# An attention and FFN kernel: every second step's probabilities through DRAM, inputs prepared in the FFN's time, first sums on GpSimd

## The chip, the core and the metric

The kernel runs on one core of a Trainium2 chip. The core has five instruction streams that matter here: TensorE (PE, matmuls), VectorE (DVE), ScalarE (ACT), GpSimd (POOL) and SyncE (SP). SP computes nothing in this kernel; its queue issues nearly all the DMA transfers, in order. Each engine runs its own instructions in order and waits on semaphores for the others. The metric is the device time of one execution, in microseconds. The median of three runs of the kernel before is 805.54 us (805.47 to 806.14).

## What is computed

The inputs are x of shape (16, 128, 1024), a context of the same shape, the weights and biases of an attention layer with 32 query heads and 8 key and value heads of 32 elements each, and a 0/1 matrix of 1024 x 1024 with one scale for the FFN. Everything is float32. Cut to what matters:

```python
def xattn(q_in, ctx):                      # q_in = layernorm(x)
    Q = q_in @ Wq + bq                     # 32 heads of 32
    K = ctx @ Wk + bk                      # 8 heads of 32
    V = ctx @ Wv + bv
    scores = einsum("bhgqd,bhkd->bhgqk", Q, K) / sqrt(32)
    w = softmax(scores, axis=-1)           # 128 x 128 for each batch and query head
    y = einsum("bhgqk,bhkd->bhgqd", w, V)
    return y.reshape(B, S, 1024) @ Wo + bo

x = x + xattn(layernorm(x), ctx)
h = layernorm(x); h[..., 819:] *= -4.0     # an inhibitory part, -0.8 / 0.2
x = x + scale * (h @ kernel)
```

## The kernel before

The 16 batches are taken in eight groups of two (`GB = 2`), numbered 0 to 7. For a group the kernel needs: the context turned so that its features lie on the partitions (`cT`), K and V from it, the normalized x turned in the same way (`xT`), Q from it, attention for two batches, the output projection, the norm, and the FFN.

**Attention steps.** A group has four attention steps, 0 to 3: batch of the pair is step mod 2, and `a` (which half of the K and V heads) is step div 2. `attend` writes one step. `scores` puts 16 small matmuls on PE, into four PSUM tiles of 128 queries x 4 heads x 128 keys. For each tile, `exponentials` takes the negated maximum on DVE (L571) and four exponentials with their sums on ACT (L575); `divide` multiplies by the reciprocal of the sums on DVE (L587), giving p. The product with V needs the keys on the partitions, so `turn` transposes p on PE, four matmuls against the identity (L592), and ACT copies the result from PSUM to SBUF (L594). When all four tiles are turned, `weighted` does four matmuls with V (L602), and ACT copies the result to `yT` (L610).

**What fills PE between.** While DVE and ACT work on the softmax of a step, PE works on other matmuls: the output projection of the group before (`out_proj`, tiles o_u, o_v, o_c), `prep_k` and `prep_v` of the next group, `prep_q` of the next group (tiles q_u, q_v, q_c), and `ffn` of the group before (tiles f, two batches). The Q product and the output projection are done with seven half-size products instead of eight (`seven`), from sums of blocks. The sums of weight blocks (`combine`, L781) are formed once, on DVE in group 0, stored to DRAM (L784) and loaded again in each group as pieces. The sums of activation blocks (L635 for the output projection) are formed in each group.

**Weight pieces.** The blocks of Wq and Wo and their sums come as pieces of 512 KB through a ring of eight buffers (`fetch`, L219). The load of a new piece is issued on SP just behind the matmul that has read the piece eight places before.

**Turning x and the context.** A context batch is loaded with its rows already spread over four partition quadrants (L157, four DMAs), and DVE then turns blocks of 32 x 32 (L343). x of groups 2 and up is normalized on DVE (L286, with the power on POOL, L285), stored to DRAM (`through_dram`, L308), loaded back by quadrants (L305) and turned on DVE (L361). The FFN's input goes the same way (`dram_f`, `turn_f`, L719).

**What sets the order.** The order is written out by hand in one Python object, `Stream`. It holds a queue of generators (pieces of dense PE work, each of which yields its nominal microseconds) and a list of events with nominal due times (`later`). `run` takes pieces from the queue until a nominal time and fires events that have come due; what is fired emits its instructions at that place in every engine's order. Nothing is reordered afterwards, so the nominal times decide who stands behind whom on each queue, SP's included. The loop at L891 adds the dense work of each group to the queue and then runs the four steps. In the steady groups (1 to 5): output projection, loads of the context two groups on, K, load of the first residual x, V, Q, FFN of the first batch of the group before, load of the second residual x, FFN of the other batch. The x of the next group is loaded and prepared from the start of the group (`get_x`), its context is turned in the first 18 nominal microseconds (`prep_ctx`). At the end of `ffn` SP stores the batch (L744); the buffer of that x is then reused for a residual load (L173), which therefore waits for the store to land.

## Time and profile before

The profiled execution took 805.76 us; its span, from first to last instruction, is 804.0 us.

| | |
|---|---|
| median of the runs | 805.54 us |
| profiled execution, and its span | 805.76 us, 804.0 us |
| TensorE clock granted | 0.996 |
| PE busy | 773.9 us (96%) |
| DVE busy | 489.1 us (61%) |
| ACT busy | 321.4 us (40%) |
| POOL busy | 71.0 us (9%) |
| one steady group (318.79 to 414.56 us) | 95.77 us, PE busy 94.52 |
| DMA moved | 190.31 MB, mean 237 GB/s |
| SP's queue, busy share of the 16 DMA engines | 72.4% |

In the profile's lines, `out<-in` names the tile written and the tiles read, `x128` is a count of instructions, then come the busy time in microseconds, the mean of one instruction in nanoseconds, and the idle time of the engine just before these instructions, with what ended it. A row of 40 digits shows the span in slices of 20 us, in tenths. In a table of stretches each row is a stretch of time, its length, the busy time and count of each engine, the granted clock, the share of the 16 DMA engines and the rate in GB/s. Timeline lines give the start, the duration, engine, line and operation. PE's instructions overlap each other, so the distance of two starts tells the cost of one better than its duration. One float32 matmul of the program appears as two instructions on PE.

### The profile page before, as it was taken

Reading aid. Unit: us, or ns where it says so; the run is one execution under the profiler, and the core shown is the slowest. Engines: PE = TensorE matmul, PEld = TensorE weight load, DVE = VectorE, ACT = ScalarE, POOL = GpSimd, SP = SyncE. Lnnn points to the kernel's source line nnn. Section 1 sums busy time; section 2 is a strip of 40 time slices with the busy share of each in tenths; the row PEclk is TensorE's granted clock in tenths of the full one; section 3 lists DMA queues with packets and bytes.
Section 4 is the critical chain, followed back from the end, with each engine's and each line's share of the span. In section 5 each row is a group of like instructions: output and inputs, shape, how many; then the busy total and the mean of one; then the engine's idle time right before and its main releaser. Section 6 shows DMA issues by size and latency. Waiting matters only on the chain.

```text
span 804.0 us, 13722 instructions
## 1 busy us (share of the span) xinstructions
PE 773.9 (96%) x5024; PEld 574.4 (71%) x5024; DVE 489.1 (61%) x910; ACT 321.4 (40%) x1257; POOL 71.0 (9%) x109
## 2 busy tenths in 40 slices
PE   3998999999999999999999999999999999999998
PEld 3886795589846897479864798548984689646556
DVE  1369756756487564866647575675647856567442
ACT  0143674344334352344433444334434445466100
POOL 1000003010010201001010100102001010100300
PEclk9999899999999999999999999999999999999999
DMA  9999499888488983889659984689847867562511
GB/s 204 360 312 319 155 372 393 265 252 270 143 283 271 249 263 140 305 252 283 208 188 293 271 264 156 244 263 261 263 158 270 293 198 260 181 214 74 197 45 79
DMA packets 98355, 190.31 MB, mean 237 GB/s; under 512 B 7888, under 2 KB 57040, under 8 KB 98288
## 3 DMA queue, kind: packets, MB, share of 16 engines
q1 hardware_dynamic: 96480, 187.73, 72.4%
q10 hardware_dynamic: 1664, 1.57, 1.1%
q8 instruction: 40, 0.66, 0.3%
q0 software_dynamic: 144, 0.14, 0.1%
q14 instruction: 27, 0.22, 0.1%
HBM read 160.04 MB, written 29.36 MB: 236 GB/s over the span
## 4 chain that ended last, share of the span: by engine, by line
PE 76%; DVE 12%; DMA 6%; issue 3%; SPq 1%; POOL 1%; ACT 0%; ACTq 0%; POOLq 0%; DVEq 0%
PE f L317 15%; PE q_u L442 13%; PE o_u L653 9%; PE q_v L442 6%; PE v L317 6%; PE tpp L592 6%; PE k L317 5%; PE o_v L653 5%; PE sc L559 4%; PE av L602 4%; PE q_c L442 3%; DVE p L587 2%; DVE st_a L277 2%; DVE x L667 2%; DVE cT L343 2%
## 5 line engine op out<-in xcount | busy, mean ns | idle before, releaser
L575 ACT ACTIVATE p<-sc,negm 128x128 f32<-128x128 f32 x512 | 181.0, 368 | 152.8 <-DVE negm L571 91.6
L594 ACT COPY pt<-tpp 128x512 f32<-128x512 f32 x128 | 74.6, 589 | 139.7 <-PE tpp L592 139.2
L571 DVE TENSOR_REDUCE negm<-sc 128x4 f32<-128x512 f32 x128 | 86.9, 681 | 38.2 <-PE sc L559 37.5
L317 PE MATMUL f<-wf_sb,x2l 128*128 128x512 f32 x256 | 105.4, 412 | 0.0
L575 ACT ACTIVATION_READ_ACCUMULATOR p<-sc,negm 128x1 f32 x512 | 105.2, 205 | 0.0
L317 PE MATMUL f<-wf_sb,x2h 128*128 128x512 f32 x256 | 101.1, 395 | 0.0
L587 DVE TENSOR_TENSOR p<-p,inv 128x512 f32<-128x512 f32 x128 | 89.8, 701 | 4.4
L179 POOL TENSOR_TENSOR x<-x,bo_b 128x256 f32<-128x256 f32 x64 | 50.2, 815 | 376.4 <-DMA x<-in_x_dram 318.5
L592 PE MATMUL tpp<-ident,p 128*128 128x128 f32 x512 | 76.8, 275 | 6.1 <-DVE p L587 4.0
L592 PEld LDWEIGHTS tpp<-ident,p 128*128 128x128 f32 x512 | 62.6, 142 | 27.6 <-issue 18.1
L442 PE MATMUL q_u<-t,piece 128*128 128x128 f32 x672 | 80.9, 275 | 0.0
L442 PEld LDWEIGHTS q_u<-t,piece 128*128 128x128 f32 x672 | 77.9, 192 | 0.0
L317 PE MATMUL v<-wv_sb,cT 128*128 128x256 f32 x256 | 63.0, 397 | 12.1 <-DMA wv_sb<-in_L_xattn_Wv_dram 12.1
L737 DVE SCALAR_TENSOR_TENSOR x<-f,fscale,x 128x512 f32<-128x512 f32 x32 | 24.0, 750 | 75.0 <-PE f L317 74.9
L653 PE MATMUL o_v<-piece,s 128*128 128x512 f32 x128 | 60.8, 601 | 2.9 <-DVE x L667 2.9
L653 PE MATMUL o_u<-piece,s 128*128 128x512 f32 x128 | 59.6, 598 | 3.4 <-DVE x L667 3.4
L317 PEld LDWEIGHTS v<-wv_sb,cT 128*128 128x128 f32 x256 | 49.6, 201 | 18.6 <-issue 12.1
L653 PE MATMUL o_u<-piece,yT 128*128 128x512 f32 x128 | 58.5, 599 | 0.0
L317 PE MATMUL k<-cT,wk_sb 128*128 128x256 f32 x256 | 57.8, 379 | 0.0
L317 PEld LDWEIGHTS f<-wf_sb,x2l 128*128 128x128 f32 x256 | 48.2, 188 | 10.9 <-issue 1.1
L317 PEld LDWEIGHTS f<-wf_sb,x2h 128*128 128x128 f32 x256 | 48.2, 188 | 10.3 <-issue 0.5
L317 PEld LDWEIGHTS k<-cT,wk_sb 128*128 128x128 f32 x256 | 48.0, 190 | 8.9 <-issue 2.6
(82 smaller groups left out, 911.9 us busy)
## 6 DMA issues: line engine op xcount, KB each, us to landing
piece<-o SPq DMA_DIRECT2D x64, 512.0 KB, 4.4
piece<-q SPq DMA_DIRECT2D x56, 512.0 KB, 5.9
piece<-in_L_xattn_Wq_dram SPq DMA_DIRECT2D x50, 512.0 KB, 5.8
piece<-in_L_xattn_Wo_dram SPq DMA_DIRECT2D x48, 512.0 KB, 4.5
xn<-in_x_dram SPq DMA_DIRECT2D x16, 512.0 KB, 5.4
x<-in_x_dram SPq DMA_DIRECT2D x16, 512.0 KB, 4.9
ctx<-in_ctx_dram SPq DMA_DIRECT2D x60, 128.0 KB, 7.3
out_dram<-x SPq DMA_DIRECT2D x15, 512.0 KB, 3.0
```

The lines of the kernel that those rows point to most:

```text
L179: lambda cut=cut: nc.gpsimd.tensor_add(x_t[:, cut], x_t[:, cut], bo_b[:, cut]) and None,
L317: nc.tensor.matmul(mm, lhsT=lhsT, rhs=rhs, start=k == 0, stop=k == n - 1)
L442: nc.tensor.matmul(mm if part is None else mm[:, part], lhsT=lhsT, rhs=rhs, start=start and n == k == 0, stop=k == len(some) - 1, skip_gro ...
L559: nc.tensor.matmul(tiles[i][:, g], lhsT=qT[rows, g], rhs=kT[rows, a, cols], start=True, stop=True,)
L571: nc.vector.tensor_reduce(negm, tile_, AX.X, ALU.max, negate=True)
L575: nc.scalar.activation(p[:, g], tile_[:, g], AF.Exp, bias=negm[:, g : g + 1], accum_out=total[:, g : g + 1],)
L587: nc.vector.tensor_mul(p, p, inv.unsqueeze(2).to_broadcast([P, NG, S]))
L592: nc.tensor.transpose(tp[:, g], p[:, g], ident)
L594: nc.scalar.copy(pt, tp)
L602: nc.tensor.matmul(mm[i * HD : (i + 1) * HD], lhsT=vs[b][:, h * HD : (h + 1) * HD], rhs=pts[i], start=True, stop=True,)
L653: nc.tensor.matmul(mm, lhsT=lhsT[:, 2 * k + c], rhs=w[:, c], start=start and k == c == 0, stop=k == c == 1, skip_group_check=True,)
L737: nc.vector.scalar_tensor_tensor(x_t[:, cut], mm, fscale, x_t[:, cut], ALU.mult, ALU.add)
```

## The change

It has three parts and the retiming that goes with them.

1. In groups 1 to 6, steps 1 and 3 don't turn p on PE. The exponentials are written so that two tiles lie interleaved in blocks of 32 keys; DVE divides and then turns 32 x 32 blocks in place; the two tiles of a pair are stored to DRAM in one DMA (`store_blocks`) and loaded back into `pT_all` with four (`fetch_blocks`), all on SP. The weighted sum of such a step is emitted 4 nominal us into the next step. A step of this kind runs for its nominal length less 1.9 us, the others for their length less 2.0. p and its transpose lie in one buffer each (`p_all`, `pT_all`) in all steps. The output projection's sums are formed in another order, s3 first, since y of step 3 now comes late.
2. The x of the group after the next is loaded, normalized and sent through DRAM in the FFN's time, step 3 (`get_x`, `rows_x`), and its context is turned there; only the last turn of x (`turn_rows`) is left for the next group. Due times of the FFN's input (`FBACK`, `late`) are moved.
3. Of the four rounds of first sums, three are formed on POOL, one stays on DVE. In group 0, Wv and Wk are loaded in two halves, the norms of x are placed among the Q product's pieces, and half of the DVE copies of the first Q are moved to ACT.

The core of the diff:

```diff
     def load_by_quadrants(dst, w, queues):
...
-        for k in range(NB):
-            queues[k % len(queues)].dma_start(out=dst[k * 32 : (k + 1) * 32], in_=src[k])
+        for h in range(2):
+            cut = slice(h * NC // 2, (h + 1) * NC // 2)
+            for k in range(NB):
+                queues[k % len(queues)].dma_start(
+                    out=dst[k * 32 : (k + 1) * 32, cut], in_=src[k][:, cut]
+                )
...
+    def rows_x(b):
...
+        normalize(by_quadrant(row), by_chunk(src), stats, f"a{b}")
+        through_dram(row, f"x{b}", 2.5, 7.0, 7.0, lambda c_t: rows.update({b: c_t}))
...
+    p_all = const.tile([P, NI, NG * S], FP, name="p_all")
+    pT_all = const.tile([P, NP, NK, 2, NG * HD], FP, name="pT_all")
+    p_dram = dram.tile([NP, NK, P, 2 * NG * HD], FP, name="p_dram")
...
+    def turn_blocks(i):
+        p = probabilities(i, True).rearrange("p g t k -> p t g k")
+        nc.vector.transpose(p, p)
+
+    def store_blocks(pair):
+        p = p_all[:, 2 * pair : 2 * pair + 2].rearrange("p i n -> p (i n)")
+        nc.sync.dma_start(
+            out=p_dram[pair].rearrange("t p n -> p t n"),
+            in_=p.rearrange("p (t n) -> p t n", t=NK),
+        )
+        stream.later(4.0, lambda: fetch_blocks(pair))
+
+    def fetch_blocks(pair):
+        for t in range(NK):
+            nc.sync.dma_start(
+                out=pT_all[t * HD : (t + 1) * HD, pair].rearrange("r k i n -> r k (i n)"),
+                in_=p_dram[pair, t].rearrange("(k r) n -> r k n", r=HD),
+            )
...
-                (1.0, 1, "a22", "a21", ADD),
-                (2.5, 2, 1, "a11", SUB),
-                (7.0, 3, "a11", "a21", SUB),
-                (9.5, 4, "a12", 2, SUB),
+                (2.0, 3, "a11", "a21", SUB),
+                (5.6, 1, "a22", "a21", ADD),
+                (6.0, 2, 1, "a11", SUB),
+                (10.0, 4, "a12", 2, SUB),
...
+                def by_vector():
+                    divide(b, a, i, total, True)
+                    turn_blocks(i)
+                    if i % 2 == 1:
+                        stream.later(2.5, lambda: store_blocks(i // 2))
...
-    def combine(w, k, part):
+    def combine(w, k, part, engine=nc.gpsimd):
...
-                nc.vector.tensor_tensor(dst[:, cols], left[:, cols], right[:, cols], op)
+                engine.tensor_tensor(dst[:, cols], left[:, cols], right[:, cols], op)
...
+        def turn_rows(grp):
+            for n, at in enumerate((30.0, 32.0, 34.0, 36.0)):
+                stream.later(at, lambda n=n: turn_x(grp * GB + n // 2, n % 2))
...
                 stream.add(
-                    once(get_x, nxt),
-                    once(prep_ctx, nxt, 3.7, 8.0, 13.0, 18.0),
+                    once(turn_rows, nxt),
                     os[grp - 1],
                     once(get_ctx, nxt + 1),
                     prep_k(nxt),
                     once(load_residual, b0, 4.0),
                     prep_v(nxt),
                     qs[nxt],
+                    once(get_x, nxt + 1),
+                    once(prep_ctx, nxt + 1, 2.5, 7.0, 11.0, 16.0),
                     ffn(p0),
                     once(load_residual, b1, 2.0),
                 )
...
-                pts = attend(b, a, length)
+                via_dram = not first and q % 2 == 1
+                us = length - 1.9 if via_dram else length
+                pending = attend(b, a, us, via_dram)
+                us -= 0.0 if via_dram else 2.0
...
+                if via_dram:
+
+                    stream.later(4.0, lambda b=b, a=a: weighted(b, a) or 1.2)
+                else:
+                    weighted(b, a)
+                    stream.now += 1.0
```

## The prediction

> **What bounds the kernel now.** I read the page first: the busy line, then the slices, then the groups that the diff touches.

> ```profile
> span 804.0 us, 13722 instructions
> PE 773.9 (96%) x5024; PEld 574.4 (71%) x5024; DVE 489.1 (61%) x910; ACT 321.4 (40%) x1257; POOL 71.0 (9%) x109
> ...
> PE   3998999999999999999999999999999999999998
> ...
> DMA  9999499888488983889659984689847867562511
> ...
> L587 DVE TENSOR_TENSOR p<-p,inv 128x512 f32<-128x512 f32 x128 | 89.8, 701 | 4.4
> ...
> L592 PE MATMUL tpp<-ident,p 128*128 128x128 f32 x512 | 76.8, 275 | 6.1 <-DVE p L587 4.0
> ```

> PE is busy 96% of the span, in every slice but the first, so PE's instruction stream is the time: a matmul taken away counts in full as long as nothing that PE needs comes late. The transposes of p (L592) are such matmuls. VectorE has room; the DMA row is near 9 in many slices and is what to distrust. I therefore cut one steady group into its four steps, from score matmuls to score matmuls:

> ```profile
> core 0: us, PE busy (x) PEld busy (x) DVE busy (x) ACT busy (x) POOL busy (x), PEclk, DMA share, GB/s
> 318.79:342.34 23.55, 22.30 (x70) 9.92 (x69) 20.01 (x37) 8.31 (x36) 2.29 (x4) 1.00 0.90 306
> 342.34:365.35 23.01, 23.01 (x136) 17.05 (x132) 13.67 (x28) 9.85 (x39) 1.09 (x2) 1.00 0.89 250
> 365.35:388.60 23.25, 23.25 (x232) 22.17 (x228) 16.55 (x28) 10.77 (x41) 4.01 (x4) 1.00 0.91 286
> 388.60:413.38 24.78, 24.78 (x176) 20.46 (x172) 10.77 (x19) 9.09 (x38) 0.98 (x2) 1.00 0.41 138
> ```

> PE has no gap in steps 1 to 3. The DMA engines are about full in steps 0 to 2 and only 0.41 busy in step 3, the FFN's time. The price of a transpose is read from PE's timeline in step 1:

> ```profile
> 354.74 0.60 PE L592 MATMUL tpp<-ident,p 128*128 128x128 f32 x4
> 355.18 1.03 PE L317 MATMUL k<-cT,wk_sb 128*128 128x256 f32 x4
> ```

> Four transposes hold PE 0.44 us, start to next start (the durations overlap, so their sum misleads).

> **The change, part by part.** The sum starts from the profiled execution's 805.8 us: 804.0 of span and 1.8 around it. The median of the runs shown, 805.5, is 0.3 below, less than matters here. A difference under 0.2% (1.6 us) can't be told from none.

> *Transposes removed.* By the order of the changed program, steps 1 and 3 of groups 1 to 6 lose their L592 rows (512 become 320): 12 steps x 4 tiles x 0.44 = **-21.1**. That certainty is why "the change does nothing" is no rival. ScalarE loses 48 copies of 0.59 us, worth nothing (40% busy, PE never waited long for it).

> *Added on VectorE.* 48 block transposes; the nearest row, turn_f L719, took 0.70 for the same shape, so 2.8 us a step, in steps with 23.0 - 13.7 = 9 and 14 us free: nothing by itself. The new access patterns (exponentials written in runs of 32, a product over 4x128, the copies of pT and yT) have no row; x2h L720, just as broken up, took 0.63 against 0.59 for the plain copy, so I take 0, with at most 0.1 us for each of 16 exponentials, 1.6 us a step, on an engine with half its time free.

> *The first group.* VectorE forms all first sums now, and PE waits for it there:

> ```profile
> PE tpp L592 <- DVE p L587: 4.0, 2, 3.4
> ```

> With 24 of 32 adds on GpSimd these 4.0 us go. GpSimd needs about 1.5 us for 512 elements (L179: 5.72 us for 7 of 256), so the three rounds take 36 us; their stores must be back before the q and o products read them, near 92 us and later, and they are begun around 44. GpSimd's power for the layer norm now queues behind up to two adds, 3 us, and VectorE behind that; VectorE has that slack once its own adds are gone. The other price shows in the timelines at 128 us, VectorE first, then GpSimd:

> ```profile
> 128.02 1.13 DVE L635 TENSOR_TENSOR s<-yT,yT 128x512 f32<-128x512 f32 x1
> ```
> ```profile
> 125.83 5.72 POOL L179 TENSOR_TENSOR x<-x,bo_b 128x256 f32<-128x256 f32 x7 [0.63 <-DMA x<-in_x_dram]
> ```

> A two-input VectorE instruction beside GpSimd took 1.13, where its like takes 0.69. [...] I take the row: VectorE saves 24 x 0.65 = 16 us in that group. Splitting Wv's load in halves lets v begin on the first half (it waited until 12.1 for all of it, and k then until 19.3 for Wk); v's end, and with it the norm of x, comes some 1.3 us sooner; the bounds are 0 and 3. Together **-5.3**.

> *What the removed matmuls covered: the handover.* Each pair of tiles now goes VectorE, store on SP's queue, landing, four fetches, landing, and only then may the weighted sum run. It stands a little into the next step, and everything on PE is queued behind it. Two rates: 512 KB lands alone in 3.0 us (out_dram, median), behind other transfers in 5.4 (dram_f) and four fetches of 128 KB in 4.8 (turn_f). [...] The queues are loaded, so I take the rows, and full engines at 306/0.90 = 340 GB/s.

> Step 1 (t from its scores): PE has scores 1.1, 8 o matmuls 6.9, k and v 13.8, scores 1.1, 14 q matmuls 3.1, so it wants pair 0 at 26.0 and pair 1 at 26.5. VectorE turns tiles 1 and 3 by about 9.4 and 15.6 (0.69 and 0.70 for each product and transpose, the o reads and the xT transposes between). On SP, four weight pieces (released at 2.8 to 8.0) and eight ctx loads stand ahead, each waiting for a lane that an earlier transfer holds; before, the ctx loads held SP 9.05 us; with dram_x and turn_x gone from this step, they end near 12. Store 0 at 12.2 lands 15.8; fetches to 17.6; store 1 at 17.7 lands 21.5; fetches 21.5 to 22.8, behind x and dram_f, land at 26.4 to 27.5. Late by 0 to 1: 0.5, six times, **+3.0**.

> Step 3, groups 2 to 5: scores, 32 q matmuls, 64 f matmuls at 0.233, scores, 4 o matmuls: pair 0 wanted at 27.7, pair 1 at 28.2. Here the diff also puts two x loads, two stores and eight fetches of x. Bytes: 138 GB/s x 24.8 us = 3.4 MB, +3.1 of x, +2.1 of p = 8.6 MB, which full engines move in 25 us. The empty step becomes full. Tiles 1 and 3 are turned by 8.2 and 14.2. Store 0 (9.5, behind two pieces and two x loads) lands 16.4; fetches; store 1 at 18.1 lands 21.8. Then SP stands at out_dram, which waits for VectorE's FFN read at about 18, now behind the x norm; the residual load behind it waits until out_dram has landed (23.3: before it was issued 3.7 us after it); then dram_x; then the fetches, 24.2 to 25.8, landed at 30. Late by **1.8**, four times: **+7.2**. In group 1 out_dram stands ahead of the fetches of pair 0 too, and there are 8 q matmuls fewer: wanted 26.5, landed 31.5: **+5.0**. Group 6 has one FFN batch, no ctx loads and no x loads: 0.

> What is late next: while PE stands, ScalarE holds yT's copy ahead of the next exponentials and VectorE the first o sum; by their rows the sums are still done 2 us before PE wants them. The weight pieces go out up to 6 us late behind turn_x; the ring of 8 pieces at 1.72 us gives 13.8, less 5 for landing. ctx and x of the next group are ready earlier than before; they were never waited for.

> Sum: 805.8 - 21.1 - 5.3 + 3.0 + 7.2 + 5.0 = **795**.

> **Rivals.** (a) *All handovers fit.* For it: step 3's share is only 0.41 now, stores alone land in 3.0, and 1.8 us is within the error of such a walk. Against: the byte count of step 3. Time: 805.8 - 26.4 = 779.
> (b) *Handovers clearly late, slower.* One mechanism: the SP queue serves in order, and the second fetch waits for out_dram's landing (step 3) or the ctx lanes (step 1). Each microsecond of mean lateness costs 12; from 26.4/12 = 2.2 us on, the change loses. At 3.2 us it is 818, at 4 it is 827. For it: shares of 0.9 in the neighbouring steps; against: PE's standing lets the transfers catch up, so lateness doesn't pile up.
> (c) *The weights starve.* If the 6 us delay and full engines use up the ring's margin, PE also waits at o pieces in step 0, some 2 us in each of five groups: 805, no change. Against it: 4 us of margin left by the above.

> **How the numbers follow.** Chances: the forecast (787 to 803) 0.40; (a) 0.22; (b) 0.29; (c) 0.09. Faster: 0.40 + 0.22 + a little of (c) = 0.63; within 0.2%: 0.04, mostly (c); slower: 0.33. The range reaches from 776, (a) with 3 us more from the start, to 818 in (b).

> **What would show it.** L592's successor at 320 transposes; PE's gap before av in steps 1 and 3 released by the pT_all DMA, under 1 us in step 1, about 2 in step 3 and 5 in group 1; a steady group of about 94.5 us instead of 95.8; DMA share about 0.9 in step 3; no wait for VectorE's p in the first 130 us. The forecast is wrong if those gaps are absent (779) or above 2.2 us in the mean, if PE waits for pieces, or if PE waits for VectorE beside GpSimd's adds in the first group.

## The result, and the profile after

The changed kernel takes 874.98 us (median of 4 runs, 869.47 to 881.08) where the kernel before takes 805.84: a ratio of 1.086, 95% interval 1.079 to 1.093. The prediction said 795 and a range to 818. The profiled execution took 881.1 us, its span is 879.3 us, 75.3 more than before.

From the page of the changed kernel: busy times, the slices of PE, of its granted clock and of DMA, and the groups that answer to those shown of before.

```profile
span 879.3 us, 13494 instructions
...
PE 795.8 (90%) x4832; PEld 573.4 (65%) x4832; DVE 517.3 (59%) x930; ACT 293.2 (33%) x1213; POOL 105.8 (12%) x133
...
PE   5988778998979899898998989899897999999998
...
PEclk9997979999989999898999989989998999999999
DMA  9988679779587897988879797797977977873321
...
L618 DVE TENSOR_TENSOR p_all<-p_all,inv 128x512 f32<-128x512 f32 x128 | 91.0, 711 | 4.4
...
L654 PE MATMUL av<-pT_all,v 128*32 128x512 f32 x256 | 53.4, 653 | 43.4 <-DMA pT_all<-p_dram 41.8
...
L624 PE MATMUL tpp<-ident,p_all 128*128 128x128 f32 x320 | 48.4, 276 | 10.3 <-DVE p_all L618 10.3
```

Two rows of the kernel before, for comparison:

```profile
PEclk9999899999999999999999999999999999999999
...
L602 PE MATMUL av<-pt,v 128*32 128x512 f32 x256 | 36.6, 605 | 0.0
```

The transposes did go from 512 to 320, and the division in its new access pattern cost nothing (711 ns, 701 before). But PE now stands (is idle, waiting) 43.4 us ahead of av, where it did not wait at all before: 3.6 us in the mean at the 12 handovers. And PE's busy time *rose*, from 773.9 to 795.8, although it has 21 us less to do by the prediction's price. The clock row says why: it has 8s and 7s where it had one 8 before (0.953 granted over the span, 0.996 before).

One steady group cut into its four steps, with the columns of the prediction's table:

```profile
351.28:381.02 29.74, 26.28 (x105) 11.29 (x104) 14.39 (x26) 8.73 (x37) 2.76 (x4) 0.89 0.94 288
381.02:403.03 22.01, 22.01 (x120) 16.13 (x116) 15.46 (x31) 7.33 (x35) 0.55 (x1) 1.00 0.76 220
403.03:433.26 30.23, 26.74 (x225) 22.97 (x224) 16.00 (x28) 9.98 (x39) 3.73 (x5) 0.89 0.90 270
433.26:457.90 24.64, 23.68 (x168) 20.02 (x164) 19.67 (x37) 7.53 (x35) 1.09 (x2) 1.00 0.73 236
```

Steps 1 and 3 are shorter or as long as before (23.0 and 24.8); what is lost stands in the steps behind them, 0 and 2, where the handover is waited for: 30 us instead of 24.7 (of which the table of before leaves out the first 1.2) and 23.3. In each of the two, 3.5 us is standing, and the clock is 0.89. PE's timeline at one of them shows both:

```profile
404.11 3.39 PE L450 MATMUL q_u<-xT,piece 128*128 128x128 f32 x28
407.43 1.05 PE L654 MATMUL av<-pT_all,v 128*32 128x512 f32 x4
411.97 1.92 PE L654 MATMUL av<-pT_all,v 128*32 128x512 f32 x4 [3.49 <-DMA pT_all<-p_dram]
413.82 1.22 PE L450 MATMUL q_u<-xT,piece 128*128 128x128 f32 x4
...
428.16 0.61 PE L450 MATMUL q_u<-t,piece 128*128 128x128 f32 x4
```

The same four matmuls with V take 1.05 us for pair 0 and 1.92 for pair 1, after 3.49 us of standing; four q matmuls take 1.22 behind it and 0.61 later. SP's queue in the same step 1 (start, time on the queue, DMA), whose scores began at 381.02:

```profile
394.46 0.31 SPq L157 DMA_DIRECT2D ctx<-in_ctx_dram  x1
395.08 0.39 SPq L636 DMA_DIRECT2D p_dram<-p_all  x1
399.76 1.73 SPq L644 DMA_DIRECT2D pT_all<-p_dram  x4
401.61 0.38 SPq L636 DMA_DIRECT2D p_dram<-p_all  x1
402.03 0.50 SPq L178 DMA_DIRECT2D x<-in_x_dram  x1
402.63 0.97 SPq L313 DMA_DIRECT2D dram_f<-x2n  x1
405.46 2.01 SPq L644 DMA_DIRECT2D pT_all<-p_dram  x4
```

By t from the scores, with the prediction's walk in brackets: last ctx load 13.4 (12), store 0 14.1 (12.2), second fetch 24.4 (21.5), landed 30.9 (26.4 to 27.5). Each link is a little later than in the walk, and it adds up to 3.4 to 4.5 us. Step 3, from 433.26:

```profile
442.22 2.13 SPq L173 DMA_DIRECT2D xn<-in_x_dram  x2
444.45 0.38 SPq L636 DMA_DIRECT2D p_dram<-p_all  x1
452.60 1.75 SPq L644 DMA_DIRECT2D pT_all<-p_dram  x4
454.46 0.38 SPq L636 DMA_DIRECT2D p_dram<-p_all  x1
454.95 0.44 SPq L805 DMA_DIRECT2D out_dram<-x  x1
459.38 0.34 SPq L178 DMA_DIRECT2D x<-in_x_dram  x1
459.77 0.43 SPq L313 DMA_DIRECT2D dram_x<-xq  x1
460.29 2.70 SPq L644 DMA_DIRECT2D pT_all<-p_dram  x4
```

Store 0 left at 11.2 (9.5) and took 8.1 us to land beside the two x loads; the second fetch, behind out_dram and the residual load that waits for it, left at 27.0 (24.2) and landed at 34.0 (30). Last, what PE waits for by releaser, where the last three rows, nearly all of them in the first 155 us, are waits that the prediction had excluded or not seen:

```profile
PE av L654 <- DMA pT_all<-p_dram: 41.8, 11, 5.4
PE tpp L624 <- DVE p_all L618: 10.3, 3, 9.7
...
PE k L322 <- DVE cT L348: 7.1, 2, 4.4
PE o_u L714 <- DVE s L696: 3.6, 1, 3.6
```

### The profile page after: what moved, and what is told of

It is laid out like the page before. It is cut to its first block, busy times and chain, and to the rows that moved or that the text cites. A ratio compares the mean times of both kernels' runs of the same rounds, so it can differ in the third digit from the quotient of the medians.

```text
span 879.3 us, 13494 instructions
## 1 busy us (share of the span) xinstructions
PE 795.8 (90%) x4832; PEld 573.4 (65%) x4832; DVE 517.3 (59%) x930; ACT 293.2 (33%) x1213; POOL 105.8 (12%) x133
## 4 chain that ended last, share of the span: by engine, by line
PE 48%; DMA 26%; DVE 8%; issue 7%; SPq 7%; POOL 3%; ACT 1%; ACTq 0%; POOLq 0%; DVEq 0%
DMA p_dram<-p_all 11%; PE o_u L714 9%; PE q_u L450 7%; PE o_v L714 6%; DMA pT_all<-p_dram 5%; PE f L322 5%; PE q_v L450 4%; PE av L654 4%; SPq L644 4%; PE o_c L714 4%; PE tpp L624 3%; PE q_c L450 3%; DMA out_dram<-x 2%; PE sc L567 2%; DMA ctx<-in_ctx_dram 2%
## 5 line engine op out<-in xcount | busy, mean ns | idle before, releaser
L600 ACT ACTIVATE p_all<-sc,negm 128x128 f32<-128x128 f32 x512 | 180.9, 371 | 279.9 <-DVE negm L597 212.4
L597 DVE TENSOR_REDUCE negm<-sc 128x4 f32<-128x512 f32 x128 | 86.5, 677 | 41.8 <-PE sc L567 41.8
L600 ACT ACTIVATION_READ_ACCUMULATOR p_all<-sc,negm 128x1 f32 x512 | 107.3, 210 | 0.0
L618 DVE TENSOR_TENSOR p_all<-p_all,inv 128x512 f32<-128x512 f32 x128 | 91.0, 711 | 4.4
L654 PE MATMUL av<-pT_all,v 128*32 128x512 f32 x256 | 53.4, 653 | 43.4 <-DMA pT_all<-p_dram 41.8
L625 ACT COPY pT_all<-tpp 128x512 f32<-128x512 f32 x80 | 46.7, 590 | 108.0 <-PE tpp L624 105.9
L322 PE MATMUL v<-wv_sb,cT 128*128 128x256 f32 x256 | 61.0, 396 | 9.4 <-DMA wv_sb<-in_L_xattn_Wv_dram 9.4
L322 PE MATMUL k<-cT,wk_sb 128*128 128x256 f32 x256 | 61.4, 401 | 7.1 <-DVE cT L348 7.1
L322 PEld LDWEIGHTS k<-cT,wk_sb 128*128 128x128 f32 x256 | 51.5, 202 | 18.3 <-DVE cT L348 8.1
L624 PE MATMUL tpp<-ident,p_all 128*128 128x128 f32 x320 | 48.4, 276 | 10.3 <-DVE p_all L618 10.3
L624 PEld LDWEIGHTS tpp<-ident,p_all 128*128 128x128 f32 x320 | 38.9, 143 | 27.8 <-issue 25.4
L322 PEld LDWEIGHTS f<-wf_sb,x2h 128*128 128x128 f32 x256 | 48.7, 190 | 10.8 <-issue 0.2
```

The costliest lines, as they stand in the source:

```text
L322: nc.tensor.matmul(mm, lhsT=lhsT, rhs=rhs, start=k == 0, stop=k == n - 1)
L597: nc.vector.tensor_reduce(negm, tile_, AX.X, ALU.max, negate=True)
L600: nc.scalar.activation(p[:, g], tile_[:, g].rearrange("p (t k) -> p t k", t=NK), AF.Exp, bias=negm[:, g : g + 1], accum_out=total[:, g : g ...
L618: nc.vector.tensor_mul(p, p, factor)
L624: nc.tensor.transpose(tp[:, g], p_all[:, i, g * S : (g + 1) * S], ident)
L625: nc.scalar.copy(pT_all[:, i // 2, :, i % 2].rearrange("p k (g q) -> p g k q", g=NG), tp.rearrange("p g (k q) -> p g k q", k=NK),)
```

## The experiments

Theory H: the loss is part 1's, at each handover a stand and the slow clock after it. Rivals: the moved x preparation, or GpSimd's sums, carry it (X); the DMA engines are simply full (B); the order on SP's queue decides (Q). All times are medians; "before" beside them was between 804.4 and 805.4 us in every comparison.

**Which part loses.** Handovers off:

```diff
-                via_dram = not first and q % 2 == 1
+                via_dram = False
```

> Theory H (handover): the loss of 69 us is part 1 alone, because at each of the 12 handovers PE stands about 3.6 us for the pT_all transfer (the groups row of the changed kernel puts 43.4 us ahead of av) and then runs its next matmuls at about half speed, 2 to 2.6 us more. With every step's probabilities turned by PE again and the other two parts kept, the time is what the prediction's sum gives without part 1: about 800 us (796 to 806), and PEclk is 1.0 throughout. Rival X (x preparation moved into step 3, or GpSimd's sums, carry the loss): the time stays above 830 us, with PE waits that no pT_all transfer ends.

823.16 us (1.023 of before, 1.021 to 1.025). So the handovers, with what they do to the rest, cost 51.8 of the 69 us, but neither theory was right: without them the kernel is still 18 us slower than before, where the sum had a gain of 5. PE has no gap over 0.8 us in the steady groups; the loss is in the first group. There VectorE's timeline, and then PE's:

```profile
99.19 0.69 DVE L618 TENSOR_TENSOR p_all<-p_all,inv 128x512 f32<-128x512 f32 x1
107.87 1.29 DVE L282 BATCH_NORM_STATS2 st_a<-xn 128x6 f32<-128x512 f32 x2 [8.00 <-DMA xn<-in_x_dram]
```
```profile
65.48 1.99 PE L322 MATMUL k<-cT,wk_sb 128*128 128x256 f32 x8 [2.77 <-DVE cT L348]
73.38 2.93 PE L322 MATMUL k<-cT,wk_sb 128*128 128x256 f32 x6 [5.91 <-DVE cT L348]
```

VectorE stood 8.00 us at the statistics of the next group's x, whose load took 7.4 us to land, and the softmax of step 3 stood behind it: PE waited 9.4 us for p. Before that, PE waited 8.7 us in all for the turned context, which VectorE turned late, behind sums that were slow beside GpSimd's.

**The two in the first group, one at a time.** The norm of x begun 16 instead of 5 nominal us after its load there, on the kernel without handovers:

```diff
-                    once(get_x, nxt + 1),
+                    once(get_x, nxt + 1, 16.0),
```

> The kernel without handovers (all probabilities turned by PE), with the norm of the next group's x begun 11 us later in the first group alone. Theory V: there VectorE stood 8.00 us at the x statistics for their load, the softmax of step 3 behind it, and PE 9.4 us for p: without that wait the time falls from 823 by 9 to 11 us, to 813. Rival: the wait for x's residual at the start of group 1 grows by as much, and the time stays at 820 or more.

811.89 us: 11.3 less, about as expected. Then the sums on VectorE too. Theory P: beside GpSimd's sums VectorE's are slow (1.6 to 1.7 us instead of 0.64, a norm of x 1.74 instead of 0.81), and this, by holding back cT, is what part 3 loses in the first group:

```diff
-    def combine(w, k, part, engine=nc.gpsimd):
+    def combine(w, k, part, engine=nc.vector):
```

> The same with the first sums on VectorE as well (parts 1 and 3 undone, part 2 kept with its first norm later). Theory P: 4 to 8 us less than with GpSimd's sums, 805 to 809 us, level with the kernel before. Rival (the sums on GpSimd relieve VectorE): 5 us more, 818 us.

805.21 us (1.000 of before, 0.998 to 1.001): 6.7 us less, and level with before. The same edit on the whole changed kernel:

> The changed kernel with the first sums back on VectorE (part 3 undone, parts 1 and 2 kept). [...] Rival, the prediction's own term (GpSimd's sums relieve VectorE): 5 us slower than the changed kernel, about 880 us.

867.14 us, 7.8 less than the changed kernel, against the rival's 880 and as theory P has it, though the runs of both kernels spread over 7 to 12 us; the 6.7 us above is the firmer figure. VectorE's piece sums in the changed kernel, with GpSimd idle and then beside GpSimd's, and GpSimd's own:

```profile
59.09 1.28 DVE L852 TENSOR_TENSOR piece<-piece,piece 128x512 f32<-128x512 f32 x2
...
65.56 3.42 DVE L852 TENSOR_TENSOR piece<-piece,piece 128x512 f32<-128x512 f32 x2
```
```profile
62.60 12.06 POOL L852 TENSOR_TENSOR piece<-piece,piece 128x512 f32<-128x512 f32 x8
```

VectorE formed eight of these sums: the four beside GpSimd's took 6.6 us, the other four 2.6. The slow ones stood ahead of cT; with all sums on VectorE, PE's wait for cT fell from 7.1 to 3.1 us in the changed kernel. So in the first group part 3 loses about 7 us and part 2 (which moves the norm) 11. With these two taken away, what is left of parts 2 and 3, with the retimed sums of the output projection, is level with the kernel before; that this level is a gain and a loss of the same size shows further down.

**One handover at a time.** The condition `q % 2 == 1` becomes `q == 1`, then `q == 3`.

> Probabilities through DRAM in step 1 alone (6 handovers), step 3 turned by PE. Theory H with each handover late by itself: 6 x (3.5 stand + 2.4 slow clock - 1.8 transposes) = +25 us over the kernel without handovers: about 825 us. Rival Q (the lateness is carried from one handover to the next by a queue that never catches up): a handover with a quiet step before it is in time, PE's stand ahead of av is under 1 us, and the time is about 790 us.

> Probabilities through DRAM in step 3 alone (6 handovers, of which the last group's has fewer loads beside it). Theory H: 6 x (3.6 + 2.4 - 1.8) = +25 us over the kernel without handovers, about 825 us, and the two halves add up to the loss of the whole change. Rival Q: under 795 us. If step 3 is worse than step 1 by more than 10 us, the x preparation that now shares its DMA counts.

822.06 and 844.87 us, that is -1.1 and +21.7 against the kernel without handovers. Step 1 alone does no harm (stands of 1.8 us at most, no slow matmul behind them), though it doesn't gain what its transposes were priced at either. That 822 meets the 825 of theory H is chance: 825 was 25 more than an expected 800, and 800 had been 823. Step 3 alone costs nearly what theory H says (+25), and together they cost 31 us more than the two apart. By PE's timeline, step 1 begins with 6 matmuls of the output projection when it is alone and with 8 in the whole change: a late av takes PE's planned time in step 0, and two matmuls slip into step 1 (read from the order; this shift was not tried by itself). With them a fourth weight piece stands on SP's queue ahead of the ctx loads (three before), so that store 0 leaves at 14.1 instead of 12.5, and the second fetch lands at 30.9 instead of 27.6. That is 3 us, but it costs more than that: stands of 1.2 to 1.8 us had no slow clock behind them, and five of the six in the changed kernel (2.1 to 4.1 us) had (where the clock fell is told in the last section).

**The slow clock by itself.** 32 useless transposes on PE ahead of every late weighted sum, into the tile that it writes afterwards (`warm` is 32 behind a handover and 0 elsewhere):

```diff
+        for n in range(warm):
+            at = mm[:, n % NK].rearrange("p g q -> p (g q)")
+            nc.tensor.transpose(at, ident, ident)
```

> The changed kernel with 32 useless transposes of the identity on PE ahead of each late weighted sum (12 places, about 3.5 us each, written where av is written afterwards): PE works where it stood. Theory C (the slow matmuls after a stand are the clock gate's answer to idling): the stands shrink to under 1 us, the matmuls after them take their usual time, and the kernel becomes faster although it does 42 us more work: about 875 - 12 x 2.3 = 847 us. Rival (the slow clock has another cause, transfers or power): the matmuls stay slow, and the time is 875 us or more.

864.55 us: faster than the changed kernel by 10 us with 42 us more work on PE (12 x 3.5, an estimate). Theory C holds in kind: the granted clock is back at 0.990, at half only in the first group, and the matmuls behind the handover take their usual time (eight with V 1.06 us, four q 0.61). The size missed (847 expected): the useless work and the 10.8 us that PE still stood are together 11 us more than the 41.8 us of stands that they replace. That an unslowed PE asks for the next handover sooner would explain it, but wasn't tested.

**SP's order or full engines.** Stores and fetches from ScalarE's queue (the store due 3.5 nominal us after its turn instead of 2.5, the fetch 5 after the store instead of 4):

```diff
-        nc.sync.dma_start(
+        nc.scalar.dma_start(
...
-            nc.sync.dma_start(
+            nc.scalar.dma_start(
```

> The changed kernel with the stores and fetches of the probabilities issued from ScalarE's queue instead of SP's. Theory Q (SP's queue serves in order: store 0 stands behind weight pieces and ctx loads, the second fetch behind out_dram, the residual load and dram_f): store 0 leaves within 1 us of its turn, PE's stand ahead of av falls under 1 us in step 1 and under 2 us in step 3, the matmuls after it keep their pace, and the time is about 825 us. Rival B (the DMA engines are full and the transfers themselves are slow): issue is earlier but landing is not, and the time stays above 860 us. ScalarE waits for landings instead, which may hold back exponentials by 1 to 2 us a step.

836.76 us: 38 less, most of the 50 that theory Q expected; the stands ahead of av that a landing ended fell from 41.8 to 17.4 us. (The due times moved too, by 1 us each, and later; that alone would not make a handover earlier.) ScalarE paid with 64.0 us of waiting for landings. Then single moves on SP's queue in the changed kernel. The residual load ahead of k, so that it isn't between store 1 and its fetches; and, in another kernel, 4 us more slack for the weighted sum of step 1:

```diff
+                    once(load_residual, b0, 4.0),
                     prep_k(nxt),
-                    once(load_residual, b0, 4.0),
```
```diff
-                    stream.later(4.0, lambda b=b, a=a: weighted(b, a) or 1.2)
+                    stream.later(8.0 if q == 1 else 4.0, lambda b=b, a=a: weighted(b, a) or 1.2)
```

> The changed kernel with one transfer moved: the residual load of step 1, which stood on SP's queue between store 1 and its fetches, is put ahead of k, so that it leaves before store 0. It asks why step 1's handovers stand 2.8 to 4.1 us here and at most 1.8 us when step 3 has none. Theory Q2 (order on SP's queue; the second fetch landed in 4.9 us behind the x load and in 3.1 without): PE's stands in step 1 fall by about 2 us, most of them under the length from which the slow clock follows, 5 x (2 + 2.4) = 22 us less: about 853 us. GpSimd's residual add also comes earlier, so rs_f and VectorE's x2n wait less. Rival (the DMA engines are too full after step 3's handover whatever the order): 868 us or more.

> The changed kernel with one number changed: the weighted sum of step 1's probabilities is put 8 instead of 4 us into step 2. Its pair 1 lands 30.9 us after the step's scores and is wanted at 26 to 27.4; with 4 us more it is in time. Theory H (a handover costs its stand and the slow clock after it, nothing else): 5 or 6 x (3.4 + 2.4) = 29 to 35 us less, about 842 us, and no slow matmuls in step 2. Rival B (full DMA engines: PE, no longer standing, asks for its weights and for step 3's handover sooner and stands there): 860 us or more.

876.84 and 868.9 us: both missed. In the first, the x load now leaves just ahead of store 0, which takes 5.8 us to land instead of 4.7, and the second fetch lands at 30.3: the contention moved. In the second, PE no longer stands at av but, for as long, at q_c; VectorE and GpSimd at that place:

```profile
504.41 1.20 DVE L291 TENSOR_SCALAR x2n<-x,mv_f,rs_f 128x1024 f32<-128x1024 f32 x1 [11.06 <-POOL rs_f L290]
505.53 0.41 DVE L411 TENSOR_TENSOR v<-v,bv_b 128x256 f32<-128x256 f32 x1
```
```profile
503.14 0.72 POOL L184 TENSOR_TENSOR x<-x,bo_b 128x256 f32<-128x256 f32 x1 [11.28 <-DMA x<-in_x_dram]
503.82 0.55 POOL L290 TENSOR_TENSOR rs_f<-ve_f,minus_half 128x1 f32<-128x1 f32 x1
```

GpSimd's residual add waits for the residual load, which SP issued behind store 1; the power for the norm stands behind the add, VectorE behind the power, and the eviction of v, which frees the PSUM tile for q_c, behind that. This second wait had run beside the first, hidden by it. Both edits together:

> The changed kernel with both edits that did little alone: step 1's weighted sum 8 instead of 4 us into step 2, and the residual load ahead of store 0. With the slack alone PE stood 3.2 to 5.7 us at q_c instead, because GpSimd's residual add waited for its load with rs_f behind it, VectorE's x2n behind that and the eviction of v behind that. Theory W (two waits side by side, each hiding the other): together the stands of step 1 go, 5 or 6 x (3.4 + 2.4) = 29 to 35 us off 875, about 843 us. Rival B (full DMA engines): 862 us or more.

851.89 us, 23 less, where the two edits alone sum to -4: theory W, short of its 29 to 35. In part that is because PE now stood 2.6 us at q_u once, and some 25 us at step 3's handovers instead of 22. Now the queue in front of the transfers. The ctx loads behind the second fetch of step 1:

```diff
-                    once(get_ctx, nxt + 1),
                     prep_k(nxt),
                     once(load_residual, b0, 4.0),
                     prep_v(nxt),
+                    once(get_ctx, nxt + 1),
```

> The changed kernel with the eight ctx loads of step 1 moved from ahead of store 0 to behind the second fetch, so that store 0 meets neither their lanes nor their bytes. Theory Q (the order on SP's queue decides in step 1): store 0 leaves at its turn, about 10 us after the scores instead of 14.1, the second fetch lands near 27 instead of 31, the stands of step 1 fall under 2 us and their slow clock goes: about 25 us less, 850 us. Rival B (moving transfers only moves the contention, as moving the residual load did): 868 us or more. The ctx blocks come later and may hold VectorE's cT in step 3.

And out_dram and the residual load behind the second fetch of step 3:

```diff
-            nc.sync.dma_start(out=out[b], in_=x_t)
+            stream.later(6.0, lambda: nc.sync.dma_start(out=out[b], in_=x_t) and None)
...
-                    once(load_residual, b1, 2.0),
+                    once(lambda: stream.later(6.5, lambda b1=b1: load_residual(b1, 1.0))),
```

> The changed kernel with out_dram and the residual load that waits for its landing put behind the second fetch of step 3 (6 and 6.5 us later in the plan). It tests the prediction's term for step 3: the fetch stood at 27.0 behind them and landed at 34.0 after the scores. Theory Q: it lands near 30, four stands fall from 4.7 to about 1 us and their slow clock goes, 4 x (3.5 + 2.4) = 24 us less: about 851 us. Rival (x's loads, stores and fetches fill step 3's DMA whatever the order): 866 us or more.

843.43 and 844.26 us, 31.5 and 30.7 less: theory Q in both. In each, the stands of the mended step fall under 1.9 us in every steady group; those of step 3 stay in the first kernel, those of step 1 grow in the second, to 6.0 us at most. Together:

> The changed kernel with both moves on SP's queue: ctx loads behind the second fetch in step 1, out_dram and the residual load behind it in step 3. Theory Q (each step's handover is late through what stands ahead of it in its own step): the gains add, 875 - 31 - 31 = 813 us. Rival N (the steps share the slack: with both handovers earlier their moved transfers meet the next handover): 830 us or more.

817.27 us, 57.7 less, and still 1.5% over the kernel before (1.012 to 1.018). The gains nearly add, and the row of av shows what is left of the 43.4:

```profile
L654 PE MATMUL av<-pT_all,v 128*32 128x512 f32 x256 | 42.4, 609 | 7.1 <-DMA pT_all<-p_dram 5.5 <-ACT pT_all L625 1.6
```

PE's busy time is 768.0 us here, with the same 4832 matmuls as the 795.8 of the changed kernel: 27.8 us less, 2.3 for each handover. Most of it is the clock: in the changed kernel PE was busy for 45.0 us at a granted clock of 0.50 behind ten of the twelve handovers, which is 22.5 us lost if half the clock doubles a matmul's time, as with the 1.22 us instead of 0.61 above; here 3.4 us behind one. The rest is probably the ends of matmuls that no next one overlaps: four with V ahead of a stand count 1.05 us, eight in a row 1.06.

**Versions that beat both.** No handover, with the four sums at their old times (and sums on VectorE, the first norm later); then with the handover of step 1 alone and its 8 us of slack:

```diff
-                (2.0, 3, "a11", "a21", SUB),
-                (5.6, 1, "a22", "a21", ADD),
-                (6.0, 2, 1, "a11", SUB),
-                (10.0, 4, "a12", 2, SUB),
+                (1.0, 1, "a22", "a21", ADD),
+                (2.5, 2, 1, "a11", SUB),
+                (7.0, 3, "a11", "a21", SUB),
+                (9.5, 4, "a12", 2, SUB),
```

> The same without any handover: the share of the sums' times alone. Theory: the 0.78 us ahead of o_u go in seven groups, 805 - 5.4 = 800 us. Rival: the wait only moves to the next operation, 804 or more.

> Handover in step 1 alone, its weighted sum 8 instead of 4 us into step 2, first sums on VectorE, the first group's norm of x later, and the four sums of out_proj at their old times. Theory: what the change was worth all along was 6 x 1.76 = 10.6 us in step 1, and the late sum costs 0.78 us in each of 7 groups (PE at o_u for s). With 4 us of slack pair 1 (landed 27.6 after the step's scores where wanted at 26) is in time: 805 - 10.6 - 5.4 + at most 2 = 789 to 793 us. Rival (the handover slows the step's other transfers, or ScalarE's and VectorE's extra work shows): 797 or more.

798.42 us (0.991, 0.989 to 0.993) and **792.80 us** (0.984, 0.982 to 0.986): both near what was expected, the second the lowest median of all. The first is 6.8 us less than the same kernel with the late sums, in which PE had waited 6.4 us for s ahead of o_u. So the late sums had cost about 7 us there, and what is left of parts 2 and 3 gains as much on the kernel before. Where is not tested; PE's waits for x ahead of o_u and o_v, 6.3 us in the kernel before, are gone, and the moved preparation of x is the likely reason. The second gains only 5.6 of the 10.6 us that its six handovers were priced at.

All handovers from ScalarE's queue, with the slack, was less good:

> Handovers in both steps, all from ScalarE's queue, the one of step 1 with the weighted sum 8 us into step 2; first sums on VectorE and the first group's norm of x later. From the 837 us of the ScalarE-queue kernel: 18 less in the first group, and the stands and slow clock of step 1 (11 + about 8 us) gone: about 800 us, which needs step 3's handovers to be in time as they were there (stands of 0.8 to 3.3 us). Rival (a handover a step earlier or later upsets the next): 815 or more.

809.8 us (1.004, 1.002 to 1.006), between the 800 expected and the rival's 815, with a spread of over 10 us in 20 runs; PE still stood 4.5 and 5.3 us at two handovers of the profiled execution. Last, the whole change with each cause taken away (both moves on SP's queue, slack in step 1, sums on VectorE, first norm later):

> All handovers of the change with every loss found so far taken away: both moves on SP's queue, step 1's weighted sum 8 us into step 2, first sums on VectorE, the first group's norm of x 11 us later. From the 817 us with both moves: 6.7 (sums) + 11.3 (norm of x) + about 5 (what step 1 still stands, with its slow clock) less: 794 us. Theory H says so if nothing else stands against the 21 us of transposes; rival: above 803, the losses of the first group were partly those of the handovers and are counted twice.

794.22 us (0.987, 0.985 to 0.990), as expected, and 4.2 us under the kernel without any handover, with the clock row full again:

```profile
span 790.4 us, 13498 instructions
...
PE 758.9 (96%) x4832; PEld 555.4 (70%) x4832; DVE 519.2 (66%) x954; ACT 292.6 (37%) x1213; POOL 71.3 (9%) x109
...
PEclk9999999999999999999999999999999999999999
```

## Why the prediction was wrong

*Transposes removed, -21.1.* Right in kind, too large: PE's busy time fell by 15.0 us in the last kernel (773.9 to 758.9), and by 7.9 for the six handovers of step 1 (771.1 to 763.2), where 10.6 were priced. Start-to-start distances priced each removed transpose, and part of that time was not given back; where it stays is open.

*What the handover adds, +3.0, +7.2, +5.0.* This is the step that failed, twice. First the lateness: "Late by 0 to 1" in step 1 and "Late by 1.8" in step 3 were 2.1 to 4.1 and, in groups 1 to 5, 3.5 to 5.4 us: 43.4 us with group 6's 1.6, in place of 15.2. The chain was named rightly link by link (ctx lanes, out_dram, the residual load), but each link was taken at its favourable end, and a landing under load (store 0 of step 3: 6.9 in the walk, 8.1 to 10.0 us in groups 2 to 5) at that of a quieter place. The count of matmuls ahead of the ctx loads came from the order of the program; that step 1's handover comes later once step 3 has one was not asked. Second, the clock: a stand was priced at its own length, and it cost PE 2.3 us more of busy time in the mean, most of it by the halved clock. Rival (b) had the mechanism of the lateness; with the mean of 3.6 us its formula gives 823, and the 27.8 us is missing from it. The 24 stores of the changed kernel took 3.4 to 10.0 us to land.

*The first group, -5.3.* Wrong in sign. GpSimd's sums cost 6.7 us: in the prediction's row a two-input instruction beside GpSimd took 1.13 instead of 0.69, a loss of 0.44; the piece sums wholly beside it lost about 1.0 each (6.6 us for four, 2.6 alone), and just these stood ahead of cT. The norm of x, with one tensor input, took 1.74 instead of 0.81 there. And part 2's first use, in group 0, put a wait for a load on VectorE ahead of the softmax: 11.3 us. The prediction followed part 2 in step 3 of the steady groups only, and "no wait for VectorE's p in the first 130 us" was the check that failed.

*Steady step 3 would have a DMA share of 0.9.* It was 0.73: 236 GB/s x 24.6 us = 5.8 MB of the 8.6 counted. Step 0 moved 8.6 MB (7.2 in the row of before), at 0.94: part of step 3's transfers left in step 0.

With the measured terms the sum closes: 805.8 - 15.0 (transposes) + 43.4 (stands) + 27.8 (PE slower behind them) + 6.7 (sums) + 11.3 (first norm) = 880.0, against 881.1 of the profiled execution. The terms come from different kernels, and the gain and the loss of about 7 us that hid each other are in none of them, so this checks the sizes and proves no single one. That the mended kernel lands on the predicted 795 is luck: it took the removal of what parts 2 and 3 had lost in the first group and of nearly all lateness, and gains smaller than the sum had.

## What to carry to other kernels

When matmuls that fill PE are replaced by a trip through DRAM, count what stands ahead of each of its transfers on the queue that issues them, and put loads that nobody waits for behind them: two such moves were worth 58 us here, and even so the twelve trips together ended only 4 us under the kernel without any. A stand of TensorE can cost more than its length, by the clock: ten of the twelve at the handovers here, 2.1 to 5.4 us long, were followed by half the clock. If taking one wait away changes nothing, look for the second one that ran beside it before giving up the theory.

## What the runs showed of the hardware

```profile
60.74:64.16 3.42, 1.97 (x40) 0.98 (x32) 2.68 (x6) 0.86 (x2) 2.28 (x3) 1.00 0.96 279
64.16:67.57 3.41, 1.99 (x8) 1.44 (x8) 3.41 (x5) 0.00 (x0) 3.41 (x3) 1.00 0.60 240
```
```profile
62.57:65.98 3.41, 0.64 (x15) 0.45 (x10) 3.30 (x4) 0.00 (x0) 3.41 (x4) 1.00 0.98 338
65.98:69.39 3.41, 3.24 (x8) 2.02 (x7) 3.41 (x4) 0.00 (x0) 3.41 (x3) 0.50 0.09 34
```
```profile
65.69 3.53 PE L322 MATMUL k<-cT,wk_sb 128*128 128x256 f32 x8 [2.77 <-DVE cT L348]
```

  Shared by two stretches (58% busy each) it left the clock alone, and the eight k matmuls behind it took 1.99 us; inside one (19% busy) it halved the clock for the next, and they took 3.53. In the same way, in the changed kernel, a stand of 1.90 us ahead of f inside one stretch (44% busy, from 236.65 us) was followed by half the clock, and one of 2.82 us ahead of av shared by two (55 and 63% busy, from 195.69 us) was not. The slow matmuls can begin after the stand, when its stretch ends: the stand that ended at 307.15 us was followed by half the clock from 308.33 on. A wholly idle stretch was not needed. Useless work that kept TensorE busy (32 transposes ahead of each late weighted sum) removed the slow clock from the handovers, and the granted clock was 0.990 over the span instead of 0.953.
- A VectorE sum of two SBUF tiles took 0.64 us alone and 1.6 to 1.7 beside GpSimd's sums (1.51 each); a norm with one such input 0.81 and 1.74.
- The handover's stores of 512 KB landed in 4.5 us in the median, but in 8.1 to 10.0 behind two loads of the same size issued 0.5 to 2.2 us earlier (step 3, groups 2 to 5).
